# A graph network's count of edges per node: comparing the low half of the destinations one column at a time

## The chip, the cores and the metric

One core of a Trainium2 chip runs the whole program in one launch. The metric is device time in microseconds of the median run. Its engines are named as in the profile: PE multiplies matrices (PEld is its weight load), DVE is the vector engine, ACT the scalar engine, POOL the third one, which here issues the gathers, and SP issues plain DMAs.

## What is computed

Two graph layers over 6250 nodes of 128 features and 200000 edges (source, destination, 16 attributes), with a residual connection around each:

```python
edge_index = jnp.stack([src, dst])
h = jnp.maximum(_layernorm(x, axis=-1), 0.0)
x = x + _L0_gnn_ref(h, edge_index, edge_attr_16, ...)   # five attention layers over the edges
h = jnp.maximum(_layernorm(x, axis=-1), 0.0)
x = x + _L1_gnn_ref(h, src, dst, ...)                   # one edge convolution, mean over each node's edges
```

Both need the number of edges of every node. In the first it divides the sum of the attributes of a node's edges, in the second it is the divisor of the mean:

```python
deg = jax.ops.segment_sum(jnp.ones_like(dst0, dtype=x.dtype), dst0, num_segments=n)
```

Only this count is touched by the change. The destinations come sorted.

## The kernel before

The edges lie on 128 partitions, 1563 columns each (CE, padded with destination -1). The program has these stages:
- **Preparation of the edges** (lines 233 to 486). Attributes are loaded 64 columns at a time (line 281, SP's queue), transposed on PE (line 290), copied by ACT (line 292), multiplied with the five layers' attention weights on PE (line 298), and written, with source and destination that POOL puts beside them (lines 301 to 303), as records to DRAM by SP and ACT (line 263). Beside it runs the count of edges per node, which the change is about. From the count follow tables that say which row of which block belongs to which node (lines 388 to 486).
- **Rows** (lines 489 to 587): POOL gathers the records in blocks by node (line 516), and the layer norm and the first layer's product run beside it.
- **Five attention layers** (lines 745 to 878) and then the **edge convolution** in its passes (lines 900 to 1117). In both POOL gathers node rows by edge (lines 791 and 945).

The count, `count` (line 202), works with a destination d as two halves: the low one, d & 127, and the high one, d >> 7, a number below NB = 49. `halves` (line 307) makes both, dlo and dhi, as bf16. For a group of G = 16 columns of edges DVE builds two one-hot blocks: `ol` (line 208) has for every edge of the group 128 comparisons of the low half with 0 to 127, `oo` (line 210) has 49 comparisons with the high half. Both are one instruction for the 16 columns: the row of numbers `iotab` is read again for each column (a broadcast over the middle dimension, `mid_bc`), and each edge's half is read again for each number (a broadcast over the last, `last_bc`). PE then multiplies the two blocks of every column (line 212), 1563 products of 128x128 with 128x49 that add up in one PSUM tile; line 213 copies it to `deg`. `ol` and `oo` have two buffers each, so the comparison of a group waits until PE is done with the group two before it.

Nothing in this stage fixes the order of the engines' work by hand: the framework's scheduler places instructions on each engine's queue, and so PE's queue holds groups of the count's products (line 212) between those of the attributes (lines 290 and 298) until the attributes are done, and then the rest of the count alone. DVE's queue holds the comparisons in turn, `ol` and `oo` of one group after the other. After the last of them come small operations of what follows (lines 322, 396, 323) and then, among others, the reductions of the layer norm (line 163) and the copy of `deg`.

`xT` (line 198) is a float32 tile of 128 x 6272, which later holds the transposed features. Here three slices of 1563 columns of it serve as scratch: fill, dstf and cum (line 273).

Of the kernel before, what the change touches and what calls it, by code (L numbers as in the profile page):

```python
# [10 lines left out]
BF = mybir.dt.bfloat16  # L11
I32 = mybir.dt.int32
AF = mybir.ActivationFunctionType
OP = mybir.AluOpType
# [7 lines left out]
P = 128  # L22
# [12 lines left out]
def gnn_kernel(ctx: ExitStack, tc: tile.TileContext, x, src, dst, ea, Ws, Wes, a_srcs, a_dsts, a_edges,  # L35
# [13 lines left out]
    nc = tc.nc  # L49
# [4 lines left out]
    CE = src.shape[1]  # L54
# [32 lines left out]
    iotab = const.tile([P, P], BF, name="iotab")  # L87
# [65 lines left out]
    def mid_bc(a, n, w):  # L153
        return a[:, None, :].to_broadcast([P, n, w])

    def last_bc(a, n, w):
        return a[:, :, None].to_broadcast([P, n, w])
# [25 lines left out]
    with tc.tile_pool(name="gat", bufs=1) as gp:  # L183
# [14 lines left out]
        xT = early.enter_context(tc.tile_pool(name="xT", bufs=1)).tile([P, NP], F32, name="xT")  # L198
# [3 lines left out]
        def count(to, lo, hi, sw, pp):  # L202

            po = pp.tile([P, NB], F32, name="po", bufs=1)
            for c in range(0, CE, G):
                n = min(G, CE - c)
                ol = sw.tile([P, G, P], BF, name="ol", bufs=2)
                nc.vector.tensor_tensor(ol[:, :n], mid_bc(iotab, n, P), last_bc(lo[:, c:c + n], n, P), OP.is_equal)
                oo = sw.tile([P, G, NB], BF, name="oo", bufs=2)
                nc.vector.tensor_tensor(oo[:, :n], mid_bc(iotab[:, :NB], n, NB), last_bc(hi[:, c:c + n], n, NB), OP.is_equal)  # L210
                for j in range(n):
                    nc.tensor.matmul(po, ol[:, j, :], oo[:, j, :], start=(c + j == 0), stop=(c + j == CE - 1))
            nc.vector.tensor_copy(to, po)
# [19 lines left out]
        with tc.tile_pool(name="sort", bufs=1) as sp, tc.tile_pool(name="sortw", bufs=2) as sw, \  # L233
# [34 lines left out]
            for k in range(K):  # L268
                o = k * (S - R) + EP * R
                n = ((k + 1) * (S - R) if k < K - 1 else K * S) - o  # L270
# [7 lines left out]
            for c in range(0, CE, EC):  # L278
                n = min(EC, CE - c)
# [3 lines left out]
                for i in range(0, n, 32):  # L283
# [4 lines left out]
                    for k, w in enumerate(ws):  # L288
                        j = i + 8 * k
# [6 lines left out]
                    for k, w in enumerate(ws):  # L296
                        j = i + 8 * k
# [13 lines left out]
                nc.vector.tensor_single_scalar(t, v, 7, op=OP.arith_shift_right)  # L311
                nc.vector.tensor_copy(hi, t)

            dlo = sp.tile([P, CE], BF, name="dlo")
            dhi = sp.tile([P, CE], BF, name="dhi")
            halves(dsti, dlo, dhi)
            count(deg, dlo, dhi, sw, pp)


# [16 lines left out]
            with tc.If(unsorted > 0):  # L336
# [7 lines left out]
                for k, bins in ((0, P), (1, NB + 1)):  # L344
                    if k:
                        for c in range(0, CE, EC):
                            n = min(EC, CE - c)
# [24 lines left out]
                    for c in range(0, CE, EC):  # L372
                        n = min(EC, CE - c)
# [7 lines left out]
                for c in range(0, CE, EC):  # L381
                    n = min(EC, CE - c)
# [70 lines left out]
            for c in range(0, Q + 1, 512):  # L453
                n = min(512, Q + 1 - c)
# [12 lines left out]
            for k in range(6):  # L467
# [4 lines left out]
                for c in range(0, Q, 512):  # L472
                    n = min(512, Q - c)
# [426 lines left out]
    with tc.tile_pool(name="ec", bufs=1) as gp:  # L900
# [10 lines left out]
        with tc.tile_pool(name="p1", bufs=2) as ep, tc.tile_pool(name="p1p", bufs=4, space=PSUM) as pp:  # L911
# [4 lines left out]
            for t in range(0, NB, 7):  # L916
                n = min(7, NB - t)
# [241 lines left out]
```

## Time and profile before

| what | value |
|---|---|
| time, median of 3 runs | 17761.48 us (17751.63 to 17762.48) |
| the profiled execution's own time | 15354.99 us |
| its span, first to last instruction | 15353.2 us |
| DVE busy over the span | 9106.1 us (59%), 14785 instructions |
| POOL busy over the span | 10194.1 us (66%), 10906 instructions |
| PE busy over the span | 3563.2 us (23%) |
| L208 `ol`, 128x2048 bf16 (the last one 128x1408) | 98 instructions, 223.4 us, mean 2280 ns |
| L210 `oo`, 128x784 bf16 (the last one 128x539) | 98 instructions, 95.2 us, mean 973 ns |
| L212 products of the count | 1563, 81.8 us |
| L208's waits for PE (L212) | 56.7 us in 21 waits |

The first table rows are of the whole program, the last four of its first 420 us, which hold the count. A row of a group gives the line of the code, the engine, the operation, the tile written and the tiles read, the shape, how often it ran, its busy time and the mean duration of one. A duration runs until the last result is written, and the next instruction of the engine can start before that; the distance from one start to the next, which the order of time shows, is what an instruction keeps its engine from the next one. The profiled execution is shorter than the timed runs, by 2406 us; no view of it says why.

### The profile page before, as it was taken

The page shows a single profiled execution, that of the slowest core. Times are in us where ns is not written, and L with a number is a line of the kernel's source. Part 1 is how long each engine was busy: PE and PEld are TensorE (multiplying, and loading weights), DVE is VectorE, ACT ScalarE, POOL GpSimd, SP SyncE. Part 2 cuts the span into 40 slices and gives each one's busy share as a digit, 9 for nine tenths or more (in the row PEclk, how much of TensorE's full clock was granted, in tenths as well). Part 3 has the DMA queues.
Part 4 walks back from the last instruction along what each step waited for, and adds up shares of the span by engine and source line. Part 5 has one row for each costly group of instructions (what it writes and reads, how often), then busy time and mean ns, then how long its engine had stood idle before and what let it go on. Part 6 is the DMA issues. An engine that isn't in the chain of part 4 may idle for free. (4 is left out here: it accounts for less than half of the span.)

```text
span 15353.2 us, 84839 instructions
## 1 busy us (share of the span) xinstructions
PE 3563.2 (23%) x18550; PEld 2269.4 (15%) x18550; DVE 9106.1 (59%) x14785; ACT 3161.7 (21%) x6154; POOL 10194.1 (66%) x10906
## 2 busy tenths in 40 slices
PE   5211111121111121111121111211111232222797
PEld 4100000010000010000010000100000111111377
DVE  8535666656666656666656666656666643333688
ACT  1221111111111111111111111111111211111476
POOL 1667777747777747777657777477777477777134
PEclk7555555555555555555555555555555555555899
DMA  3212222222222222222222222222222333333665
GB/s 123 61 50 71 67 67 67 66 64 67 66 67 67 64 62 67 67 67 67 60 66 67 67 67 67 57 70 67 67 67 66 91 117 111 111 113 112 230 231 192
DMA packets 722984, 1301.20 MB, mean 85 GB/s; under 512 B 207200, under 2 KB 503552, under 8 KB 682624
## 3 DMA queue, kind: packets, MB, share of 16 engines
q0 software_dynamic: 329600, 663.87, 17.7%
q1 hardware_dynamic: 356416, 587.30, 11.5%
q10 hardware_dynamic: 36416, 44.22, 0.9%
q8 instruction: 159, 2.61, 0.1%
q14 instruction: 393, 3.22, 0.1%
HBM read 1094.17 MB, written 200.45 MB: 84 GB/s over the span
## 5 line engine op out<-in xcount | busy, mean ns | idle before, releaser
L791 POOL DMA_INDIRECT g<-table,srci x8240 | 7780.3, 944 | 2565.9 <-issue 2490.9
L810 PE MATMUL xp<-ident,z 128*128 128x128 f32 x2060 | 507.2, 427 | 7548.2 <-DVE z L807 7548.2
L804 DVE TENSOR_TENSOR mt<-g,ael 128x32 f32<-128x32 f32 (+1 forms) x260 | 57.1, 219 | 3563.2 <-DMA g<-table,srci 3532.1
L945 POOL DMA_INDIRECT g<-btable,srci x1648 | 1573.0, 954 | 502.7 <-issue 478.8
L854 DVE TENSOR_REDUCE ys<-pr 128x1032 f32<-128x4128 f32 (+1 forms) x260 | 1841.4, 7082 | 8.8
L810 PEld LDWEIGHTS xp<-ident,z 128*128 128x128 f32 x2060 | 403.6, 223 | 7728.6 <-DVE z L807 7326.7
L866 PE MATMUL op<-y,oh 128*128 128x387 bf16 x2060 | 840.2, 511 | 1528.5 <-DVE ys L867 848.1
L850 DVE TENSOR_TENSOR pr<-g,mt 128x4128 f32<-128x4128 f32 (+1 forms) x260 | 1147.2, 4412 | 70.5 <-ACT mt L847 70.5
L872 ACT COPY sv<-st 128x260 f32 x2060 | 834.6, 405 | 1272.5 <-DVE u L821 1118.4
L867 DVE TENSOR_REDUCE ys<-op 128x258 f32<-128x774 f32 x1030 | 998.8, 970 | 105.7 <-PE op L866 81.9
L858 ACT CAST y<-ys 128x1032 bf16<-128x1032 f32 (+1 forms) x260 | 265.1, 1020 | 3825.7 <-DVE ys L857 3825.7
L960 DVE TENSOR_TENSOR xe<-g,ar 128x512 f32<-128x512 f32 x412 | 282.0, 687 | 1115.5 <-DMA g<-btable,srci 1115.3
L856 ACT CAST y<-ys 128x1032 bf16<-128x1032 f32 (+1 forms) x260 | 264.5, 1017 | 2816.7 <-DVE ys L854 2816.7
L516 POOL DMA_INDIRECT rg<-rec_d,rowi x412 | 468.1, 1136 | 419.6 <-ACT neqw L533 273.6
L963 PE MATMUL xps<-ident,xe 128*128 128x128 f32 x1648 | 441.7, 424 | 1239.4 <-DVE xe L960 1239.4
L869 DVE SCALAR_TENSOR_TENSOR st<-st,cor,ys 128x129 f32<-128x129 f32 x2055 | 710.6, 346 | 9.4
L966 ACT ACTIVATE sq<-xps,negc 128x512 f32<-128x512 f32 x412 | 281.6, 686 | 1699.1 <-DVE xs L964 1698.4
L963 PEld LDWEIGHTS xps<-ident,xe 128*128 128x128 f32 x1648 | 294.2, 216 | 1418.3 <-issue 1405.0
L866 PEld LDWEIGHTS <-oh 128*128 128x128 bf16 x2060 | 200.0, 119 | 1937.7 <-issue 850.3
L813 DVE TENSOR_REDUCE tm<-xp 128x8 f32<-128x1024 f32 (+1 forms) x260 | 315.7, 1214 | 238.2 <-PE xp L810 238.2
L1089 POOL COPY A<-st 128x256 f32 x412 | 248.5, 603 | 313.2 <-DVE st L1086 297.2
L861 ACT ACTIVATE oh<-neq,onesq 128x1024 bf16<-128x1024 bf16 (+1 forms) x260 | 296.1, 1139 | 475.3 <-PE op L866 428.7
(389 smaller groups left out, 9385.0 us busy)
## 6 DMA issues: line engine op xcount, KB each, us to landing
g<-table,srci POOLq DMA_INDIRECT x8240, 2.5
e_d<-xs SPq DMA_DIRECT2D x103, 1024.0 KB, 4.3
x<-e_d SPq DMA_DIRECT2D x103, 1024.0 KB, 4.8
e<-e_d SPq DMA_DIRECT2D x103, 1024.0 KB, 4.9
neq<-neq_d SPq DMA_DIRECT2D x255, 256.0 KB, 3.1
eqt<-eqt_d SPq DMA_DIRECT2D x255, 256.0 KB, 2.7
g<-btable,srci POOLq DMA_INDIRECT x1648, 2.5
table<-hb SPq DMA_DIRECT2D x80, 195.0 KB, 2.5
```

Of the source, the lines that this page charges most:

```text
L516: nc.gpsimd.indirect_dma_start(out=rg[:, j, :, :].rearrange("p k r -> p (k r)"), out_offset=None, in_=rec_d, in_offset=bass.IndirectOffset ...
L791: nc.gpsimd.indirect_dma_start(out=g[:, j, :], out_offset=None, in_=table, in_offset=bass.IndirectOffsetOnAxis(ap=srci[:, c0 + j:c0 + j + ...
L810: nc.tensor.transpose(xp[:, j, :], z[:, j, :], ident)
L813: nc.vector.tensor_reduce(tm[:, :n], xp[:, :n], AX.X, OP.max)
L850: nc.vector.tensor_tensor(pr.rearrange("p q k d -> p (q k) d")[:, :w], g[:, :w, :D + 1], last_bc(ex, w, D + 1), OP.mult)
L854: nc.vector.tensor_reduce(y, pr[:, :n].rearrange("p q k d -> p q d k"), AX.X, OP.add)
L866: nc.tensor.matmul(op[:, j, :3 * (D + 1)], oh[:, h + j, :], y3[:, h + j], start=True, stop=True)
L867: nc.vector.tensor_reduce(sm, op[:, :, :3 * (D + 1)].rearrange("p b (a d) -> p b d a", a=3), AX.X, OP.add)
L869: nc.vector.scalar_tensor_tensor(st[:, j, :D + 1], state[0][:, :D + 1], cor[:, j:j + 1], sm[:, j - h, :], op0=OP.mult, op1=OP.add)
L872: nc.scalar.copy(svf[:, ds(r[j], 2 * HW)].rearrange("p (a w) -> p a w", a=2), mid_bc(st[:, j, :], 2, HW))
L945: nc.gpsimd.indirect_dma_start(out=g[:, j, :], out_offset=None, in_=btable, in_offset=bass.IndirectOffsetOnAxis(ap=srci[:, c0 + j:c0 + j + ...
L963: nc.tensor.transpose(ps[:, k, :], xe[:, k, :], ident)
```

## The change

The low half's comparison is made column by column. Each instruction compares `iotab` with one number per partition, the edge's low half[...]. Therefore `dlo` is float32 now and lies in a fourth slice of `xT` (4 x 1563 = 6252 of its 6272 columns). The high half, the products, the two buffers of `ol` and all later stages are written as before. In the changed file all lines below 208 are one higher.

```diff
             for c in range(0, CE, G):
                 n = min(G, CE - c)
                 ol = sw.tile([P, G, P], BF, name="ol", bufs=2)
-                nc.vector.tensor_tensor(ol[:, :n], mid_bc(iotab, n, P), last_bc(lo[:, c:c + n], n, P), OP.is_equal)
+                for j in range(n):
+                    nc.vector.tensor_scalar(ol[:, j, :], iotab, lo[:, c + j:c + j + 1], None, op0=OP.is_equal)
                 oo = sw.tile([P, G, NB], BF, name="oo", bufs=2)
...
-            dlo = sp.tile([P, CE], BF, name="dlo")
+            dlo = xT[:, 3 * CE:4 * CE]
             dhi = sp.tile([P, CE], BF, name="dhi")
             halves(dsti, dlo, dhi)
             count(deg, dlo, dhi, sw, pp)
```

In the compiled order of the changed kernel DVE's queue holds 16 comparisons of `ol` and then one of `oo` for each group; the first of the 16 carries the waits, the other 15 none. PE's queue holds 416 of the count's products before the last attribute products and 1147 behind them (448 and 1115 before the change).

## The prediction

> **What bounds the kernel now.** I read the page first, for the weights. Its chain of waits reaches only the last 73 us and doesn't touch the lines changed, so I went on to where lines 208 to 212 run: the busy time in stretches, then who waits for whom, then the instructions in order of time. The edit lives in the first 390 us of a span of 15353.2 us, so what matters is which engine ends that part.
>
> The answer by stretches; the DVE column and the last three (PE's granted clock, DMA share, GB/s) carry it:
>
> ```profile
> core 0: us, PE busy (x) PEld busy (x) DVE busy (x) ACT busy (x) POOL busy (x), PEclk, DMA share, GB/s
> 28.00:72.00 44.00, 33.10 (x265) 31.65 (x266) 35.11 (x25) 7.70 (x15) 7.43 (x15) 1.00 0.79 260
> 72.00:178.00 106.00, 105.67 (x759) 103.76 (x759) 57.92 (x37) 30.01 (x57) 34.09 (x53) 1.00 0.77 264
> 194.00:300.00 106.00, 28.34 (x551) 27.00 (x548) 106.00 (x69) 0.00 (x0) 0.00 (x0) 0.50 0.00 1
> 300.00:390.00 90.00, 23.92 (x464) 23.02 (x465) 90.00 (x60) 0.00 (x0) 0.00 (x0) 0.50 0.00 1
> ```
>
> Two regimes. From 72 to 178 us PE is busy for 105.67 of 106.00 us: the count's products share it with the transposes and products of the edge attributes, and DVE has slack. From 178 to 390 us the attributes are done, no DMA runs, ACT and POOL stand still, and DVE is busy all the time. POOL's first gather of rows starts only at 449.82 us, behind this. So in the second regime every microsecond on DVE is one of the whole time, in the first none is until DVE's slack is used up.
>
> The order of time at the count's end (start, duration):
>
> ```profile
> 384.75 2.29 DVE L208 TENSOR_TENSOR ol<-iotab,dlo 128x2048 bf16<-128x2048 bf16 x1
> 386.95 0.97 DVE L210 TENSOR_TENSOR oo<-iotab,dhi 128x784 bf16<-128x784 bf16 x1
> 387.84 1.62 DVE L208 TENSOR_TENSOR ol<-iotab,dlo 128x1408 bf16<-128x1408 bf16 x1
> 389.38 0.72 DVE L210 TENSOR_TENSOR oo<-iotab,dhi 128x539 bf16<-128x539 bf16 x1
> 390.00 0.15 DVE L322 CAST nxf<-nxi 127x1 f32<-127x1 int32 x1
> 390.07 0.28 DVE L396 TENSOR_SCALAR upto<-iota,pcol 128x128 f32<-128x128 f32 x1
> 390.26 0.15 DVE L323 TENSOR_SCALAR xT<-nxf 128x1 f32<-128x1 f32 x1
> ```
>
> Durations overlap, so I cost by start to start. The compare of 16 columns holds DVE for 386.95-384.75 = 2.20 us, 0.1375 us a column; the high half takes 0.89. A group repeats every 3.087 us: 68 of them fill 177.88 to 387.84 us.
>
> **What a column costs after.** 98 instructions of 2048 elements go, 1563 of 128 elements come: a comparison with one float32 number per partition, bf16 in and out. The nearest rows have this very form, but in float32: L396 above (0.19 us to the next start), and
>
> ```profile
> 17.97 0.27 DVE L81 TENSOR_SCALAR ident<-iota,pcol 128x128 f32<-128x128 f32 x1
> 18.17 0.31 DVE L88 CAST iotab<-iota 128x128 bf16<-128x128 f32 x1
> ...
> 421.10 0.45 DVE L460 TENSOR_SCALAR woh<-xa,pcol 100x444 f32<-100x444 f32 x1
> 421.47 0.37 DVE L462 TENSOR_SCALAR tbi<-xa 1x444 int32<-1x444 f32 x1
> ...
> 437.70 0.38 DVE L486 TENSOR_SCALAR keep<-new 128x444 f32<-128x444 f32 x1
> 437.99 2.28 DVE L500 TENSOR_TENSOR cm<-iota,t0E 128x2048 bf16<-128x2048 f32 x1
> ```
>
> L486 has constants for operands and holds DVE for 0.29 us; L460, as wide, takes its operand from a column and holds it for 0.37. So a column operand costs 0.06 to 0.08 us more. The rate without it: L311 (1563 elements) starts at 26.50 and its successor at 27.39, 0.89 us; L424 (50 elements) takes 0.09; the slope is 0.80/1513 = 0.53 ns an element, the intercept 0.065. With a column operand the fixed part is 0.19 - 0.068 = 0.122, 0.20 - 0.068 = 0.132 and 0.37 - 0.235 = 0.135 us. I take 0.130. Nothing suggests that the next instruction fetches its column under the running one: these instructions followed others just as closely and still paid.
>
> What 128 bf16 elements cost on top no row shows; L310 and L312 write bf16 but read int32. The bounds are 0.068 us, the rows' rate, and 0.033, twice that: the Trainium skill, "VectorE: DVE Perf Modes", section "The perf-mode tier table", gives tensor_scalar from bf16 in SBUF four elements a cycle and float32 two. The float32 rows agree with the latter (0.53 ns), and their operand column didn't cost them the rate, so I take four for bf16: 0.130 + 0.033 = **0.163 us a column**, against 0.1375. By the rows' rate it would be 0.198.
>
> The same page, section "The TRN2 errata", speaks against the change and for it. It says that many small tiles each pay a fixed part and advises 512 elements or more, which the edit goes below; but it prices the part at 58 cycles, so a column would cost (58+32)/0.96 = 94 ns, less than now. The row that bears on it (0.122 to 0.135 us fixed, with a column operand) decides for me: 94 ns would make the sum below -44 us, the row makes it +34.
>
> **The sum.** The compiled order of the changed kernel leaves 1147 count products behind the last attribute product on PE, 1115 now: two groups move to the second regime. DVE then has 71 groups left there (1131 columns), 69 now.
> - Now: 177.88 to 390.00 us.
> - PE's part before it loses 32 products; the first regime's groups of 16 take 0.88 us: -1.8 us.
> - The first three groups precede the attribute products on PE. Each takes 16 x (0.163-0.1375) = 0.4 us longer: +1.2 us, so DVE goes free at 177.3 us.
> - 1131 x 0.163 = 184.4 us, high halves 70 x 0.883 + 0.62 = 62.4 us.
> - End: 177.3 + 184.4 + 62.4 = 424.1 us: **+34 us**.
>
> What I cost at nothing: in the first regime a group takes 16 x 0.163 + 0.88 = 3.5 us of PE's 5.745 us period (L208 starts at 94.50, 100.25 and 106.00); the cover is PE, and without it the other 27 groups add 0.4 us each, 11 us. PE's products in the second regime (0.8 us a group) hide under DVE as now. The low half is written as float32 instead of bf16, by the same cast (0.96 us); at worst it takes L274's 2.35 us, +1.4. It lies in spare columns of xT, whose next writers are later than the count already. The 1465 added instructions have to be fetched; nothing else uses the DMA there (share 0.00), so I take nothing; if DVE waited even 10 ns for each of the 1131, +11. The only wait per group stays at its first compare, for PE; no queue but DVE is passed. Later work keeps its order, moved by the same amount.
>
> In the profiled execution: 15355.0 (span 15353.2 and 1.8 around it) + 34 = 15389. The median shown is 2406 us longer than the profiled execution; no view says where, so I carry the difference in us: 17761.5 + 34 = **17796**. If the missing time stretched all work alike (17761/15355 = 1.157), +39.
>
> **The rivals.** Delta = 1131c - 150.4 us, c the cost of a column; break-even at c = 0.133 us.
> - *Likeliest*, four a cycle and a paid column operand: fixed 0.122 to 0.140, c 0.155 to 0.173, +25 to +45 us. 62%.
> - *Two a cycle*: bf16 goes no faster than the float32 rows because the operand is four bytes: c 0.190 to 0.206, +64 to +83: at 0.198, 17835. For: the only rates that the trace shows. Against: the page's table. 20%.
> - *Faster*: in a run of like instructions the operand's fetch is overlapped, leaving the constant form's 0.065 fixed: c = 0.098, -40 us, 17722; at the page's 94 ns, -44. The place is the start-to-start gap on DVE after 178 us; it decides below 0.133. For: each column operand is known long ahead. Against: L81, L396, L460. 12%.
> - *One a cycle*: c = 0.130+0.133 = 0.263, +147 us; 17909. The rows at two speak against it. 3%.
> - *It does not do what it says*: the compares cost as much as now, or something else ends the part; 0 to +5. DVE at 106.00 of 106.00 us speaks against. 3%.
>
> **How the numbers follow.** 0.2% is 35.5 us, about what a measurement of this kernel can tell from no change. The likeliest case straddles it (c = 0.164 is the edge): I give 32 of its 62 to slower, 30 to within. Slower: 32+20+3 = 55%. Within: 30, 3 of the faster case where part of the fetch stays, and 3: 36%. Faster: 9%. Range: the first two cases, 17785 to 17845, 82%; the likeliest alone 17786 to 17807.
>
> **What would show it.** In the changed profile: L209 as 1563 TENSOR_SCALAR, start to start near 0.163 us, duration near 0.24; the high half's 0.97 us unchanged; DVE still full and PE waiting for it from about 178 us; L322's start near 424 us instead of 390.00; 72 to 178 us still PE's. I am wrong on the size if the gap is near 0.2, on the sign if it is below 0.133, and on the whole argument if DVE idles after 178 us or the first regime grows by more than some microseconds.

## The result, and the profile after

| | before | changed |
|---|---|---|
| time, median of 15 runs each, on the same chips | 17755.50 us | 17796.72 us (17789.62 to 17809.12) |
| ratio | | 1.0022, 95% interval 1.0015 to 1.0030 |

The change costs 41 us; the interval reaches from 27 to 53. By stretches of the changed kernel's profile (busy us and instructions of PE, its weight load, DVE, ACT and POOL, then PE's granted clock, the DMA share and GB/s):

```profile
72.00:178.00 106.00, 101.13 (x720) 99.32 (x721) 62.07 (x296) 29.90 (x56) 11.68 (x54) 0.97 0.80 274
194.00:300.00 106.00, 25.14 (x489) 22.09 (x487) 106.00 (x520) 0.00 (x0) 0.00 (x0) 0.50 0.00 1
390.00:420.00 30.00, 6.60 (x128) 5.82 (x128) 30.00 (x146) 0.00 (x0) 0.00 (x0) 0.50 0.00 1
```

The same two regimes: up to 178 us PE is nearly full (101.13 of 106.00) and DVE has slack, then DVE is full (third column), and stays so beyond 390 us. The count's end in the order of time:

```profile
416.62 2.68 DVE L209 TENSOR_SCALAR ol<-iotab,xT 128x128 bf16<-128x128 bf16 x16
419.22 0.96 DVE L211 TENSOR_TENSOR oo<-iotab,dhi 128x784 bf16<-128x784 bf16 x1
420.11 2.68 DVE L209 TENSOR_SCALAR ol<-iotab,xT 128x128 bf16<-128x128 bf16 x16
...
426.02 0.14 DVE L323 CAST nxf<-nxi 127x1 f32<-127x1 int32 x1
```

The 16 comparisons hold DVE for 419.22 - 416.62 = 2.60 us, 0.163 us each, where the one instruction took 2.20; a group repeats every 3.49 us instead of 3.087. The operation after the count starts at 426.02 us instead of 390.00.

### The profile page after: what moved, and what is told of

Its sections match the earlier page's. It is cut to its first block, busy times and chain, and to the rows that moved or that the text cites. A ratio compares the mean times of both kernels' runs of the same rounds, so it can differ in the third digit from the quotient of the medians.

```text
span 17796.6 us, 86306 instructions
## 1 busy us (share of the span) xinstructions
PE 3498.6 (20%) x18550; PEld 2277.4 (13%) x18550; DVE 9129.1 (51%) x16250; ACT 3177.6 (18%) x6154; POOL 10158.8 (57%) x10906
## 5 line engine op out<-in xcount | busy, mean ns | idle before, releaser
L843 DVE TENSOR_REDUCE am<-mt 128x16 f32<-128x48 f32 (+1 forms) x260 | 53.7, 207 | 3552.4 <-remote 3428.0
L965 DVE TENSOR_SCALAR_CACHE_REDUCE xs<-xps,negc 128x512 f32<-128x512 f32 x412 | 308.5, 751 | 1498.0 <-remote 1093.6
L857 ACT CAST y<-ys 128x1032 bf16<-128x1032 f32 (+1 forms) x260 | 264.3, 1017 | 2785.3 <-DVE ys L855 2017.4
L964 PE MATMUL xps<-ident,xe 128*128 128x128 f32 x1648 | 379.9, 407 | 1517.2 <-DVE xe L961 1439.1
L1076 PE MATMUL rps<-fs,e 128*128 128x128 f32 x3296 | 386.9, 276 | 4.4 <-DMA e<-e_d 4.4
```

Source lines behind the costliest of these rows:

```text
L964: nc.tensor.transpose(ps[:, k, :], xe[:, k, :], ident)
L1076: nc.tensor.matmul(ps[:, k, :], es[:, K * q + k, :], fs, start=True, stop=True)
```

## The experiments

**e1: is the shorter execution another count?** The kernel before, unchanged, profiled again.

> The kernel before, unchanged, profiled again. Theory: the 2406 us by which its first profiled execution was shorter than the timed runs has nothing to do with the count; whatever the span is this time, L322 starts at 390.0 us within 1 us, the group of the count repeats every 3.087 us, and the missing time lies in the layers' gathers, behind 440 us. Rival: the long executions are slower in the count too; then L322 starts later than 390 by up to 1.157 times, 451 us, and the +36 us read from the two profiles is wrong.

Measured: span 17737.3 us. L322 starts at 390.35 us and the group repeats every 3.087 us. The rival falls: the count takes the same time in both. The difference lies behind it; the earlier, short execution and then this one:

```profile
600.00:3000.00 2400.00, 320.13 (x2047) 189.47 (x2048) 1328.22 (x2300) 451.98 (x1132) 1774.49 (x1820) 0.50 0.25 65
```
```profile
600.00:3000.00 2400.00, 280.26 (x1885) 169.64 (x1885) 1118.79 (x1987) 399.93 (x1021) 1524.77 (x1556) 0.50 0.22 57
```

In the same 2400 us POOL (fifth column) issues 1820 operations, nearly all gathers, and then 1556, though a gather takes the same time (944 and 946 ns). In e1 POOL waits 295.3 us of this stretch, in 18 waits, for DVE's product L850, which reads the gathered rows; the short execution has no such wait. In the 48 runs of the kernel before that belong to e5 to e8 it took 15343 us, so the kernel does not make the difference. That the chip makes it is not shown: the chip of e1 to e4 and that of e5 to e8 carry the same number, 4. What makes the loop slower stays open.

**e2: what makes up 0.163 us?** Six forms of the comparison, added to the changed kernel behind the count:

```diff
+            for j in range(8):
+                nc.vector.tensor_scalar(q1[:, j, :], iotab, dlo[:, j:j + 1], None, op0=OP.is_equal)
+            for j in range(8):
+                nc.vector.tensor_scalar(q2[:, j, :], iotab, 3.0, None, op0=OP.is_equal)
...
+                nc.vector.tensor_scalar(q6[:, j, :], wb, dlo[:, j:j + 1], None, op0=OP.is_equal)
```

> The changed kernel with six forms of the comparison added behind the count, on scratch tiles that nothing reads: bf16 128 wide with an operand column, bf16 128 with a constant, float32 128 with a column, float32 128 with a constant, bf16 512 and bf16 2048 with a column. Theory (fixed 0.065 us, 0.065 more for an operand column, four bf16 elements a cycle): start to start 0.163, 0.098, 0.197, 0.132, 0.263 and 0.663 us. Rival 1 (two a cycle and a smaller fixed part of 0.096): 512 wide 0.363, 2048 wide 1.16. Rival 2 (the operand column costs nothing, small instructions have a floor of 0.16): the constant form takes 0.163 as well.

From the order of time on DVE (start, time of the whole row, count at the end; L498 compares with a column, L500 with a constant, both bf16; L502 and L504 the same in float32; L506 and L508 wider, with a column):

```profile
430.73 0.25 DVE L498 TENSOR_SCALAR q<-iotab,xT 128x128 bf16<-128x128 bf16 x1
430.89 0.15 DVE L329 TENSOR_TENSOR un<-un 128x1 f32<-128x1 f32 x1
...
439.27 0.28 DVE L500 TENSOR_SCALAR q<-iotab 128x128 bf16<-128x128 bf16 x2
439.47 0.18 DVE L429 CAST mX<-ni 128x49 f32<-128x49 int32 x1
```
```profile
443.29 0.47 DVE L502 TENSOR_SCALAR q<-iota,xT 128x128 f32<-128x128 f32 x2
443.68 1.16 DVE L504 TENSOR_SCALAR q<-iota 128x128 f32<-128x128 f32 x8
444.76 0.60 DVE L506 TENSOR_SCALAR q<-wb,xT 128x512 bf16<-128x512 bf16 x2
...
445.96 0.34 DVE L506 TENSOR_SCALAR q<-wb,xT 128x512 bf16<-128x512 bf16 x1
446.22 0.62 DVE L459 TENSOR_TENSOR xa<-xa 128x444 f32<-128x444 f32 x1
...
447.54 0.75 DVE L508 TENSOR_SCALAR q<-wb,xT 128x2048 bf16<-128x2048 bf16 x1
448.21 0.45 DVE L461 TENSOR_SCALAR woh<-xa,pcol 100x444 f32<-100x444 f32 x1
```

Start to start, by dividing: bf16 with a column 0.16, with a constant 0.20/2 = 0.10; float32 with a column 0.39/2 = 0.195, with a constant 1.08/8 = 0.135; 512 wide 446.22-445.96 = 0.26, 2048 wide 0.67 us. From 128 to 2048 elements that is 0.51/1920 = 0.27 ns each, half of the 0.53 that the float32 rows showed at two elements a cycle, and so the four a cycle of the prediction. All six lie within 0.01 us of the theory; rival 1 would have needed 1.16 us for the widest, and rival 2 0.16 for the constant. The operand column costs 0.06 us an instruction in both types, and repeating the same instruction hides none of it: the 16 in a row of the changed kernel stand 0.163 us apart.

**e3: two instructions a column.**

```diff
-                    nc.vector.tensor_scalar(ol[:, j, :], iotab, lo[:, c + j:c + j + 1], None, op0=OP.is_equal)
+                    for h in (0, P // 2):
+                        nc.vector.tensor_scalar(ol[:, j, h:h + P // 2], iotab[:, h:h + P // 2], lo[:, c + j:c + j + 1], None, op0=OP.is_equal)
```

> The changed kernel with each column compared in two instructions of 64 elements. Theory: what a column costs is the fixed part of 0.130 us for 0.033 us of elements, so a column takes 0.293 us and the 1131 columns of the second regime add 1131 x 0.130 = 147 us over the changed kernel: L323's place near 573 us, time near 17940; the first regime still hides it (5.6 of 5.745 us a group), perhaps with some us more. Rival (the time goes with the elements): as the changed kernel, 17797.

Measured: 17999.4 us, ratio to before 1.0143 (1.0127 to 1.0159), so 256 us more, the next operation (L324 in this file) at 624.14 us. The price was right, the place not:

```profile
614.74 4.76 DVE L210 TENSOR_SCALAR ol<-iotab,xT 128x64 bf16<-128x64 bf16 x32
619.41 0.97 DVE L212 TENSOR_TENSOR oo<-iotab,dhi 128x784 bf16<-128x784 bf16 x1
620.29 3.30 DVE L210 TENSOR_SCALAR ol<-iotab,xT 128x64 bf16<-128x64 bf16 x22
```

32 instructions take 4.67 us, 0.146 each and 0.292 a column: 0.293 was expected, so the fixed part decides and not the elements. But the compiled order left 1307 products behind the attributes (1147 in the changed kernel); the expectation had kept 1147. Ten more groups of 5.56 us are the missing 51 us, nearly. How many groups the scheduler puts beside the attributes depends on the comparison's form.

**e4: the other half of the change alone**, dlo as float32 in xT, compared 16 columns at a time:

```diff
-            dlo = sp.tile([P, CE], BF, name="dlo")
+            dlo = xT[:, 3 * CE:4 * CE]
```

> The kernel before with the second half of the change alone: the low half as float32 in xT's spare columns, still compared 16 columns in one instruction. Theory: this costs nothing; the instruction of 2048 elements keeps its 2.20 us, the count ends at 390 us, the time is that of before within 10 us. Rival: the four-byte operand or its place has a share in the 41 us; then the compare is longer than 2.28 us and the time up to 41 us above before.

Measured: 17749.41 us, ratio 1.0004 (0.9995 to 1.0012); the count ends at 390.55 us, the instruction takes 2285 ns. The theory holds: no cost, the place being 0.2 us behind e1's. Whether a bf16 column would have served as well, no run tries.

**e5 and e6: where the columns stand.** The comparison by columns in the first 28 groups, or in the other 70:

```diff
-                for j in range(n):
-                    nc.vector.tensor_scalar(...)
+                if c < 28 * G:          # e6: c >= 28 * G
+                    for j in range(n):
+                        nc.vector.tensor_scalar(...)
+                else:
+                    nc.vector.tensor_tensor(ol[:, :n], mid_bc(iotab, n, P), last_bc(lo[:, c:c + n], n, P), OP.is_equal)
```

> The changed kernel with the comparison by columns in the first 28 groups alone, which stand beside the attributes; the other 70 compare 16 columns in one instruction, as before. The compiled order puts 1147 count products behind the last attribute product, as in the changed kernel. Theory: the columns themselves are hidden under PE; only the two groups that moved behind cost, 2 x 3.09 - 1.8 (32 products less on PE) + 1.2 (three groups at the start): L323's place near 396 us, time +6 us over before. Rival (a column costs 0.0255 us more wherever it stands): 448 x 0.0255 = +11 us on top, place near 407.

> The changed kernel with the comparison by columns in the last 70 groups alone, the first 28 as before. The compiled order puts 1115 count products behind the last attribute product, as before the change. Theory: 69 groups (1099 columns) are in the regime that DVE bounds, 1099 x 0.0255 = +28 us: place near 418.5 us, time +28 over before; with the run of the first 28 groups this adds up to the change. Rival (the whole +36 is the columns' price, the moved groups nothing): place near 426, time +36 to +41.

Measured: e5 ratio 1.0002 (0.9994 to 1.0011), +3 us; e6 1.0017 (1.0010 to 1.0024), +27 us. Their next operations (L326 in both files):

```profile
400.92 0.14 DVE L326 CAST nxf<-nxi 127x1 f32<-127x1 int32 x1
```
```profile
421.50 0.13 DVE L326 CAST nxf<-nxi 127x1 f32<-127x1 int32 x1
```

The times agree with the theory (+6 and +28), but their intervals reach from -9 to +17 and from 15 to 38 us and so hold the rivals too (+17, +36). Both places are 3 to 5 us later than the theory said. In e5 that is no clear verdict from the place, 400.92 lying midway between 396 and 407. The cause of the lateness can be read on PE: in these two runs an attribute product (L302) takes 407 ns in the mean, in the first profile of before 394. The last attribute product starts at 184.5 and 184.2 us, 179.6 there; so both places shift by some 4.6 us, whatever is compared. Taking it off leaves 396.3 and 416.9. What DVE does behind its last wait for PE needs no such estimate: e5 takes 215.2 us for 70 groups (185.71 to 400.92), e6 236.1 us for 68 (185.41 to 421.50). That is 3.087 and 3.49 us a group, with the shorter last one, as the theory has it.

**e7, e8, e9: the other way to a cheaper comparison.** Keep one instruction for 16 columns, but lay a block out with the columns inside, so that all its operands run with step one: both blocks (e7), the high half (e8), the low half (e9).

```diff
+    iotax = const.tile([P, P, G], BF, name="iotax")
+    nc.vector.tensor_copy(iotax, iota[:, :, None].to_broadcast([P, P, G]))
...
-                ol = sw.tile([P, G, P], BF, name="ol", bufs=2)
-                nc.vector.tensor_tensor(ol[:, :n], mid_bc(iotab, n, P), last_bc(lo[:, c:c + n], n, P), OP.is_equal)
+                ol = sw.tile([P, P, G], BF, name="ol", bufs=2)
+                nc.vector.tensor_tensor(ol[:, :, :n], iotax[:, :, :n], mid_bc(lo[:, c:c + n], P, n), OP.is_equal)
...
-                    nc.tensor.matmul(po, ol[:, j, :], oo[:, j, :], ...)
+                    nc.tensor.matmul(po, ol[:, :, j], oo[:, j, :], ...)
```

> The kernel before with both one-hot blocks laid out the other way round, numbers outside and the 16 columns inside, against a constant block of the numbers: the same single instruction for 16 columns, but all three operands run with step one in bf16. PE reads weights and moving columns with a step of 16 elements. Theory: two elements a cycle, a group takes 2048 x 0.26 + 0.07 = 0.6 us at four, 1.14 us at two for the low half and 0.48 for the high, 1.62 us against 3.09; DVE no longer bounds, PE does: 178 us and 1115 products of 0.055 us, at most 240 us for the count's end, time about 17600. Rival (a step of 32 bytes slows the weight load[...]): 1563 x 0.22 + 115 us of attributes, the count ends near 470, time +80.

> The kernel before with the high half alone laid out the other way round (only the moving operand has a step). The compiled order leaves 1035 products behind the attributes. Theory: the high half takes 0.48 us for 0.89, a group 2.20 + 0.48 = 2.68 us; from about 182 us 65 groups, the count ends near 356 us, time -34 us. Rival (tensor_tensor stays at one element a cycle): the group keeps its 3.09 us and the time its place within 10 us.

> The kernel before with the low half alone laid out the other way round: the weights have a step of 16 elements, the moving operand none. The compiled order leaves 980 products behind the attributes. Theory (the moving operand's step was what doubled a product on PE, 0.05 to 0.10 us, in the two runs before; the weights' step costs little): a group takes DVE 1.14 + 0.89 = 2.03 us; 8 groups more in the attributes cost 7 us; from 187 us 61 groups, the count ends near 311 us, time -79 us against before. Rival (the weights' step costs as much): a product stays at 0.10 us, the attributes end 25 us or more later, and the time is at most 60 us below before.

| | ratio to before | gain | deg copied at (before 397.2 to 398.9 us) | first gather of rows (before 449.8 to 451.5 us) |
|---|---|---|---|---|
| e7, both | 0.9940 (0.9927 to 0.9954) | 90 us | 320.5 us | 361.4 us |
| e8, high half | 0.9990 (0.9983 to 0.9997) | 15 us | 380.2 us | 435.1 us |
| e9, low half | 0.9950 (0.9937 to 0.9964) | 92 us | 326.6 us | 367.5 us |

On DVE all three did what they should. The kernel before, e7, e8 and e9 in the second regime:

```profile
384.89 0.82 PE L212 MATMUL po<-oo,ol 128*128 128x49 bf16 x16 [2.26 <-DVE oo L210]
```
```profile
257.98 3.33 PE L214 MATMUL po<-oo,ol 128*128 128x49 bf16 x32 [0.19 <-DVE oo L212]
```
```profile
256.14 1.62 PE L214 MATMUL po<-oo,ol 128*128 128x49 bf16 x16 [1.06 <-DVE oo L212]
258.21 0.56 DVE L212 TENSOR_TENSOR oo<-iotax,dhi 128x784 bf16<-128x784 bf16 x1
258.68 2.29 DVE L210 TENSOR_TENSOR ol<-iotab,dlo 128x2048 bf16<-128x2048 bf16 x1
```
```profile
255.38 1.22 DVE L210 TENSOR_TENSOR ol<-iotax,dlo 128x2048 bf16<-128x2048 bf16 x1
255.51 1.14 PE L214 MATMUL po<-oo,ol 128*128 128x49 bf16 x16 [0.87 <-DVE oo L212]
256.51 0.97 DVE L212 TENSOR_TENSOR oo<-iotab,dhi 128x784 bf16<-128x784 bf16 x1
```

The low half takes 1.13 to 1.14 us instead of 2.20, the high 0.47 instead of 0.89. What I missed is PE: 32 products take 3.33 us in e7, 0.104 each, against 0.82/16 = 0.051 before. A step of 16 elements in the moving operand doubles a product (e8, with that step alone, has 0.101), the step in the weights alone adds 0.02 (e9: 0.071). The clock is not the cause: from 230 to 300 us it was 1.00 in e7 and e8, and 0.50 in e9 and before. In the first regime, which PE bounds, this is paid at once: the last attribute product starts at 223.7, 208.5 and 202.4 us in e7, e8 and e9, against about 180 before, also because 705, 528 and 583 of the count's products precede it (448 before). So e7 gained 90 of the 150 us expected and e8 15 of 34. In e9, with the cheap step alone, the time gained 92 us (64 to 112) where 79 were expected, though its count ends 15 us later than the 311 expected, since the attributes end at 202 and not at 187 us.

The cheaper comparison is not the whole of these gains. On DVE the count ends at 319.0 us in e7 and 325.7 in e9, 71 and 66 us earlier than in before and e10. But two steps of the layer norm, 6.7 us each, which stood behind the count (L163 and L165), have been placed beside the attributes by the scheduler (at 67.5 and 95.2 us in e7, 56.3 and 150.7 in e9), and from the count's end to the first gather of rows it is 42 us instead of 60. In e10 and then e9:

```profile
451.53 1.29 POOL L516 DMA_INDIRECT rg<-rec_d,rowi  x1 [276.29 <-ACT neqw L533]
```
```profile
367.53 1.30 POOL L518 DMA_INDIRECT rg<-rec_d,rowi  x1 [173.24 <-ACT neqw L535]
```

That gather comes 88, 15 and 84 us earlier in e7, e8 and e9, which agrees with the times. e7 and e9 beat both kernels; between themselves the intervals do not part them.

**e10 and e11: before and changed once more, side by side on one chip.**

> The kernel before once more, as the neighbour on the same chip of the next run and of the run above. Theory: L322 within 390 to 396 us, depending on how long one attribute product takes in this execution (394 to 407 ns so far), the group at 3.087 us.

> The changed kernel once more beside it on the same chip. Theory: the place of L323 is 34 to 37 us behind that of the neighbour's L322; of it 71 groups times 0.40 us, and 2 groups more behind the attributes; start to start of L209 0.163 us.

```profile
391.69 0.15 DVE L322 CAST nxf<-nxi 127x1 f32<-127x1 int32 x1
```
```profile
430.47 0.44 DVE L323 CAST nxf<-nxi 127x1 f32<-127x1 int32 x1
```

38.8 us apart, 2 more than expected; times 17767.09 and 17799.73, one run each. An attribute product takes 394 ns in the mean in e10 and 407 in e11, which puts the last one 5.0 us later (181.5 and 186.5 us). The difference lies in one stretch: in e10, as in both first profiles, e1 and e4, some 40 of these products between 160 and 190 us take about 280 ns instead of 414 (55 to 58 of all 392); in e2, e3, e5 to e9 and e11 only 20 to 24 of the 392 are so short. The clock records of the five that have it hold a stretch of 10.24 us at full clock that begins about then; but e6 shows the full clock throughout without such products, so that column alone does not decide it. With one instruction for 16 columns beside the attributes four of eight executions have the stretch (before, e1, e4, e10; e6 to e9 not), with columns there one of five (the first changed profile; e2, e3, e5, e11 not). If it is the change's doing, it costs up to 5 us that the first changed profile does not contain. These runs can't decide that; it stays open.

## Why the prediction was right, point by point

**A column's price** was the step that decided, and it was right: 0.163 us forecast and measured. e2 shows why: 0.033 us for 128 elements at four a cycle, 0.07 of every instruction, 0.06 for the operand column. So of the page that the prediction names (the Trainium skill, "VectorE: DVE Perf Modes") the rate in the section "The perf-mode tier table" held. The price in the section "The TRN2 errata", 58 cycles and the elements, from which the prediction worked out 94 ns, did not: even with a constant the instruction takes 0.10 us, with the column 0.163. The rival that the column is fetched under the running instruction, and the one with two elements a cycle, have fallen in e2. The 512 or more elements that the same section advises are the right instinct here: e3 halves them and pays another 0.13 us a column.

**The sum**, step by step against e1 and the changed profile, by the count's place (+35.7 us; +34 forecast):
- Groups that DVE bounds: 3.49 for 3.087 us in 68 of them, 27 us; forecast 28 for 69.
- Two groups more behind the attributes: 2 x 3.49 = 7.0 us, as forecast. e5 and e6 part the two terms: the two groups and the columns beside the attributes move the time by 3 us (-9 to +17; the place, freed of PE's difference, says 6), the columns behind them by 27 (15 to 38).
- DVE goes free in the changed kernel at 182.95 us with 70 groups left, in e1 at 181.31 with 68: 1.6 us later, where I had 0.6 us earlier. This is the term that was off, by 2.2 us; with 0.7 us less than forecast in the first term, the place is some 1.6 us later than the sum said. e10 and e11 show that this end moves by up to 5 us between executions.

**What was costed at nothing.** The float32 half cost nothing (e4). The first regime hid its columns (e5; DVE waited for PE 53.5 us in it, 56.7 before). Fetching 1465 more instructions shows nowhere: the gap is 0.163 us to the end, DVE has no idle time behind 194 us. Later stages kept their order: from the count's end to the first gather of rows it is 60 us in both kernels.

**From the place to the time.** The first gather of rows starts at 450.43 us in e1 and 486.01 in the changed kernel, so the 36 us of place reach the stages behind undiminished. They stand against 41 us of time, whose interval begins at 27: the 5 us between them lie within it. The longer attribute products of e11 would be of that size, but whether they belong to the change is what e10 and e11 left open. Carrying the microseconds over, not the ratio 1.157, was right, since e1 has the same count in a long execution.

The forecast number stood 0.19% above before, the measured one is at 0.23%: the likeliest case held, and on the side of 0.2% to which I gave a little more, though the interval (0.15 to 0.30%) reaches to both sides. That 17796 was met to the microsecond is luck: it started from a median that was 6 us higher, and the interval is 26 us wide.

## What to carry to other kernels

Cost a DVE loop of small instructions by start to start, with a row that has the same kind of operand: here a per-partition operand costs as much again as the fixed part and twice the 128 elements. Sixteen instructions of 128 elements lost here to one of 2048 (2.60 against 2.20 us), though each of their elements costs a quarter (0.27 against 1.07 ns): the fixed part outweighs that. Giving the one instruction operands of step one halved it (1.14 us) and ended the count 66 to 71 us earlier; the rest of the 90 us gained came from where the scheduler then put the layer norm. Before turning a layout for one engine, price the step on the engine that reads it, and look at which of the two bounds each stretch; and count in the compiled order how much work moves from one stretch to the other: in e3 ten groups did, worth some 51 us.

## What the runs showed of the hardware that I had not expected

- A moving operand read with a step of 16 bf16 elements doubled a product of 128x49 (0.051 to 0.101 us); weights with the same step cost 0.02 us.
- POOL's copies beside the comparison got faster with the change. L301's 25 copies took 889 ns in the mean before, the same copies (L302) 353 after, 300 to 430 ns where DVE was not comparing. POOL was busy for 34.09 of 106 us and then 11.68. e6, with the two-tensor comparison in this stretch, has 33.55, e5 with columns 12.82. It bought nothing, POOL bounding nothing there.
- The same kernel took 15343 us in the runs beside e5 to e8 and 17740 to 17770 in all others; a short and a long execution (15353.2 and 17737.3 us) have a count of the same length. The cause is open.
